# A planned four-layer graph-attention kernel: the first graph's start in tiles and plain products, and due times as priorities

## The chip, the cores and the metric

The kernel runs on one core of a Trainium2 chip. The metric is device time in microseconds (us) of one execution, and lower is better. "PE" is TensorE, "DVE" VectorE, "ACT" ScalarE, "POOL" GpSimd and "SP" SyncE, which here only issues transfers. All arithmetic is float32, except for adjacency codes in bf16 and 16-bit halves of float32 numbers that are moved as raw bits.

## The reference

There are 32 independent graphs (`B = 32`) of 512 nodes (`N`) with 256 features (`H`), each with a 512x512 adjacency matrix of integers. Each graph passes through four residual layers, one after another. Every layer normalises its input first:

```python
h = jnp.maximum(_layernorm(x, axis=-1), 0.0)
x = x + layer(h, adj, weights)
```

Layer 0 is what the change touches. Its attention matrix is used twice:

```python
q = einsum('bnh,hk->bnk', h, att_W)
score = einsum('bnk,bmk->bnm', q, h) / sqrt(H)
att = softmax(score + mask)            # mask from adj
for W, b in ((W0, b0), (W1, b1)):
    h = tanh(att @ (h @ W + b))
```

Layers 1 and 2 are graph attention with additive scores (a leaky ReLU of a source term plus a target term, masked, softmax or normalised exponentials, times the projected features). Layer 3 has bilinear scores, a softmax and two more products.

## The kernel before

**Tiles.** A graph's `x` is held as four tiles of 128 nodes (`NT = 4`), and features as two chunks of 128 (`HC = 2`). For a product PE needs the normalised features turned, as `hT` (features on partitions). In `normed` (L464 and on) DVE takes the statistics of a tile (`stats`, L470 and L471) and the variance of two tiles (`variance`, L474), POOL raises it to the power -1/2 (`root`, L477), DVE makes an offset (`offset`, L480), and ACT applies both (`norm`, L484). Then DVE splits the tile into two planes of 16-bit halves (`split`, L489), a transposing transfer on SP's queue turns them (`turn`, L492) and ACT joins the halves into `hT` (`join`, L497).

**Seven products for eight.** Layer 0's features `fa0` (`features_t`, PE L676), values `v0` (`by_nodes`, PE L702) and similarities `q0` (`scores0`, PE L729) are each computed as a 2x2 block product with seven multiplications (`seven`). For this DVE forms block sums of the operands (`block_sums`, L561: `hs` and `fs`), the weights are laid out in seven blocks (`seven_of`, L343 to L348), and partial results are added up: L691 for `fa`, L714 and L719 for `v`, L746 for `q`. Then come the exponential (ACT L737 or L743), the mask (DVE L752), `attend` (PE `bank_a`, L659: attention times values, in two groups of four steps), tanh (ACT L765), and the second convolution (`bank_z` L774, `bank_o` L792). The next layer's first product is `bank_v` (L591). Layer 3 uses the same scheme (`f3`, `v3`, `s3`, `w3`).

**The plan.** No loop over graphs is executed in order. `graph(b, ...)` only records operations, each with an engine, a cost (how long it holds the engine, and how long until its result is there), the operations it comes after, and the buffers it uses (35 pages, 8 PSUM banks, one adjacency buffer, and so on). `Plan.order` then plays the costs through: whenever an engine is free it takes the ready operation of lowest rank whose buffers are free. The result is written out as one fixed instruction order per engine. `Plan.best` tries several spacings between graphs (`APART`) and keeps the shortest plan. Five graphs are in flight at a time. The rank before is

```python
o["rank"] = ((o["graph"] - late) * apart + late * apart_last - o["way"], o["number"])
```

where `way` is the longest path of costs from the operation to the end of its own graph; paths that lead into another graph do not count. On the chip only the order stands; what an instruction waits for are the tiles that it reads or overwrites.

**Transfers.** SP's queue holds the loads of `x` (`fetch_x`, L437, 512 KB at once), of the adjacency (`fetch_adj`, L440, 256 KB each, one after another) and the transposing transfers of `code` (L452) and of the planes (L492). ACT's queue starts with `b0` (L365), `att_W` and `W0` (L367). All other weights are loaded by POOL (`load`, L290) and prepared by PE (`transposed`, L310; `product`, L327) and DVE (L313, L331). In the plan each transfer has a fixed duration, and transfers do not slow each other.

Of the kernel before, what the change touches and what calls it, by code (L numbers as in the profile page):

```python
# [19 lines left out]
P = 128  # L20
# [28 lines left out]
D_X, D_ADJ, D_ADJ0 = (550.0, 5000.0), (550.0, 12000.0), (550.0, 2500.0)  # L49
# [3 lines left out]
class Plan:  # L53
# [9 lines left out]
    APART, APART_LAST = [1000.0 * k for k in range(32, 64, 2)], [1000.0 * k for k in (2, 8)]  # L63
    SLACK = {"V": (1.05, 0.0), "A": (1.05, 0.0), "G": (1.5, 0.0), "D": (1.0, 800.0)}
# [4 lines left out]
    def op(self, engine, cost, after, emit, graph, uses=()):  # L69

        much, more = self.SLACK.get(engine, (1.0, 0.0))
        cost = cost[0] * much, cost[1] * much + more
        flat = []
        for a in after:
            flat += a if isinstance(a, tuple) else [a]
        o = {"engine": engine, "cost": cost, "after": [a for a in flat if a is not None], "emit": emit,
             "graph": graph, "uses": list(uses), "number": len(self.ops)}
        self.ops.append(o)
        return o
# [6 lines left out]
    def best(self, pools):  # L86
        apart = min(itertools.product(self.APART, self.APART_LAST), key=lambda a: self.order(pools, *a)[1])
        out, took = self.order(pools, *apart)
        assert len(out) == len(self.ops), "the plan is stuck"
        return out, took  # L90

    def order(self, pools, apart, apart_last):
        free = {pool: list(range(n)) for pool, n in pools.items()}
        users = {}
        for o in self.ops:
            o["left"], o["way"] = len(o["after"]), 0.0
            for p in o["uses"]:
                p["users"] = 0
                p.pop("number", None)
            for a in o["after"]:  # L100
                users.setdefault(a["number"], []).append(o)
# [4 lines left out]
        for o in reversed(self.ops):  # L106
            o["way"] += o["cost"][1] + self.PASS
            late = max(0, o["graph"] - last + 2)
            o["rank"] = ((o["graph"] - late) * apart + late * apart_last - o["way"], o["number"])
            for a in o["after"]:  # L110
                if a["graph"] == o["graph"]:
                    a["way"] = max(a["way"], o["way"])
# [8 lines left out]
        now, out = 0.0, []  # L121
        while True:
            for e in engines:
                skipped = []
                while at[e] <= now and ready[e]:
                    rank, o = heapq.heappop(ready[e])
                    new = [p for p in o["uses"] if "number" not in p]
                    need = [p["pool"] for p in new]
                    if any(len(free[n]) < need.count(n) for n in need):
                        skipped.append((rank, o))  # L130
                        continue
                    for p in new:
                        p["number"] = free[p["pool"]].pop(0)
                    holds, until = o["cost"]
                    at[e] = now + holds
                    out.append(o)
                    heapq.heappush(events, (at[e], next(numbers), None))
                    heapq.heappush(events, (now + until + self.PASS, next(numbers), o))
                for x in skipped:
                    heapq.heappush(ready[e], x)  # L140
# [19 lines left out]
def kernel(  # L160
# [118 lines left out]

    W = Tiles("w")  # L280

    def prepare(engine, cost, after, emit, *keys):
        return plan.op(engine, cost, after, emit, 0, W.uses(keys))

# [3 lines left out]
    def load(dst, src, *keys):  # L288

        return prepare("G", G_LOAD, [], lambda: nc.gpsimd.dma_start(out=dst() if callable(dst) else dst, in_=src), *keys)  # L290
# [73 lines left out]
    w0_sb, att_sb = raw("raw9"), raw("raw10")  # L364
    nc.scalar.dma_start(out=b0_sb, in_=line_of(b0))  # L365
    for n, dst, w, key in (("att", att_s, att_w, "raw10"), ("w0", w0_s, w0, "raw9")):
        a = prepare("A", (500.0, 4000.0), [], lambda w=w, key=key: nc.scalar.dma_start(out=raw(key)(), in_=rows_of(w)), key)  # L367
        ready[n] = seven_of(raw(key), dst, HALF, [a], key)
# [45 lines left out]
    def graph(b, adj_before, x_before):  # L414
# [4 lines left out]
        def op(engine, cost, after, emit, *keys):  # L419
            return plan.op(engine, cost, after, emit, b, T.uses(keys))  # L420
# [15 lines left out]
        def fetch_x():  # L436
            nc.sync.dma_start(out=T["x"], in_=x[b].rearrange("(t p) h -> p t h", p=P))  # L437
# [4 lines left out]
        got_x = op("D", D_X, [x_before], fetch_x, "x", "ahead")  # L442
        got_adj = [adj_before]
        for t in range(NT):

            got_adj.append(op("D", D_ADJ if b else D_ADJ0, got_adj[-1:], partial(fetch_adj, t), "adj"))
# [18 lines left out]
        def normed(l, xs):  # L465
# [28 lines left out]

            def join(t):
# [5 lines left out]
            for g in range(NT // 2):  # L501
# [4 lines left out]
                for t in (2 * g, 2 * g + 1):  # L506
                    flat, over = f"planes{l}_{t}", f"planesT{l}_{t}"
                    a = op("A", A_NORM, [r], partial(norm, t), "x", f"xn{l}")
                    a = op("V", V_SPLIT, [a], partial(split, t), f"xn{l}", flat)
# [95 lines left out]
        def leaky_exp_t(l, ss, sign):  # L605
# [35 lines left out]
            else:  # L641
                a = op("V", V_SQUARES, ss, squares, f"sT{l}")
                a = op("D", D_OUT, [a], collect, f"sT{l}")
                a = op("D", D_SPREAD, [a], spread, key)
# [59 lines left out]


        hs = normed(0, [got_x] * NT)
        right_after, right = block_sums("hs0", "hT0", lambda j, l, T=T: T["hT0"][:, j, half(l)], hs, left=False)
        qs = features_t(0, right_after, right, att_s, ready["att"])

        def block_v0(i, l):  # L710
            return T["v0"][:, two(l), LEAD + i * HALF : LEAD + (i + 1) * HALF]

        def write_v0(i, l, key, start, after):
            return op("V", V_SUM, after, lambda: nc.vector.tensor_tensor(  # L714
                block_v0(i, l), two_tiles(key, start, HALF),
                b0_sb[:, i * HALF : (i + 1) * HALF].unsqueeze(1).to_broadcast([P, 2, HALF]), ALU.add), key, "v0")

        def add_v0(i, l, key, start, after):
            return op("V", V_SUM, after, lambda: nc.vector.tensor_tensor(  # L719
                block_v0(i, l), block_v0(i, l), two_tiles(key, start, HALF), ALU.add), key, "v0")  # L720

        vs = seven("v0", pe(nt=4), lambda x, after=right_after: after(x) + ready["w0"], ("hT0", "hs0"),
                   partial(by_nodes, w0_s, right), write_v0, add_v0, beside=N // 2)
        vs = [tuple(vs.values())] * NT
        left_after, left = block_sums("fs0", "fa0", lambda i, j: T["fa0"][:, j, half(i)], qs, left=True)

        def scores0(right, left, x, p, fresh):
            for j in range(2):
                nc.tensor.matmul(p[:, j * N // 2 : (j + 1) * N // 2], right(x)[:, j * P : (j + 1) * P], left(x),  # L729
                                 start=fresh and j == 0, stop=True, skip_group_check=True)  # L730


        def block_e0(i, l):
            return T[f"e0_{l}"][:, :, half(i)]

        def exp0(i, l, key=None):
            nc.scalar.activation(block_e0(i, l), two_tiles(key, 0, N // 2) if key else block_e0(i, l), AF.Exp,  # L737
                                 scale=float(H) ** -0.5)

        def write_q(i, l, key, start, after):  # L740
            if (i, l) == (1, 0):
                return op("A", A_COPY, after, partial(exp0, i, l, key), key, f"e0_{l}")
            return op("A", A_COPY, after, lambda: nc.scalar.copy(block_e0(i, l), two_tiles(key, 0, N // 2)), key, f"e0_{l}")  # L743

        def add_q(i, l, key, start, after):
            a = op("V", V_MASK, after, lambda: nc.vector.tensor_tensor(  # L746
                block_e0(i, l), block_e0(i, l), two_tiles(key, 0, N // 2), ALU.add), key, f"e0_{l}")
            exps.append(op("A", A_EXP, [a], partial(exp0, i, l), f"e0_{l}"))
            return exps[-1]

        def masked0(i, l):
            nc.vector.tensor_tensor(block_e0(i, l), block_e0(i, l), T["mask0"][:, two(l), half(i)], ALU.mult)  # L752

        exps = []
        qb = seven("q0", pe(n256=4), lambda x, right_after=right_after, left_after=left_after: right_after(x) + left_after(x),
                   ("hT0", "hs0", "fa0", "fs0"), partial(scores0, right, left), write_q, add_q)
        es = {il: op("V", V_MASK, [a, m0], partial(masked0, *il), "mask0", f"e0_{il[1]}") for il, a in qb.items()}
        es = [(es[0, c // 2], es[1, c // 2]) for c in range(NT)]

# [257 lines left out]
        op("G", G_STORE, last, store, "y3", "slot", "ahead")  # L1017
        return code, got_x

    code, got_x = None, None  # L1020
    for b in range(B):
        code, got_x = graph(b, code, got_x)
# [37 lines left out]
```

## Time and profile before

| | |
|---|---|
| Median of 3 timed runs | 2427.62 us (2426.65 to 2427.65) |
| The profiled execution's own time | 2423.93 us |
| Its span, from the first to the last instruction | 2422.2 us |
| Busy share of the span: PE, DVE, ACT, POOL | 98%, 85%, 71%, 10% |
| DMA, mean over the span | 73 GB/s |

The durations below are from the profiled execution. Its span lies 1.7 us below its own time and 5.4 us below the median of the timed runs, so a change of the span is carried over to the median as a difference. A matmul in float32 shows as two records (two passes). Their recorded ends are modelled and overlap the next one: the cost of a pass on a busy PE is the distance between starts, for example 0.87 us for the four passes of one `bank_a` step, and not the recorded 0.38 us each.

### The profile page before, as it was taken

What the parts mean: (1) busy time and instruction counts of PE and PEld (TensorE: products, weight loads), DVE (VectorE), ACT (ScalarE), POOL (GpSimd) and SP (SyncE); (2) the same over time, 40 slices, a digit from 0 to 9 for tenths busy, and PEclk for the clock granted to TensorE, in tenths of its full rate; (3) what the DMA queues carried; (4) which work ended last, traced back from release to release, by engine and by line L of the source; (5) the groups of instructions that cost most, each with busy time, mean ns of one, the idle gap of its engine ahead of it and who ended that gap; (6) DMA issues with size and microseconds to landing.
All of it is one profiled execution on the core that took longest, in us unless ns stands there. A gap on an engine that the chain in (4) does not pass through costs nothing.

```text
span 2422.2 us, 36547 instructions
## 1 busy us (share of the span) xinstructions
PE 2372.1 (98%) x11660; PEld 1988.7 (82%) x11660; DVE 2059.8 (85%) x6333; ACT 1727.2 (71%) x3393; POOL 252.0 (10%) x320
## 2 busy tenths in 40 slices
PE   6999999999999999999999999999999999999998
PEld 5777788888888888888888888888888888887877
DVE  6677888888988888988888988889888898886888
ACT  3666767777777777777777777777777777665885
POOL 2000101010101010011001011001010110000110
PEclk9999999999999999999999999999999999999999
DMA  6222333324333333333233333333333333320221
GB/s 165 58 53 64 74 68 92 75 62 88 77 77 85 72 63 83 77 79 77 67 78 77 76 83 70 64 85 77 77 82 75 62 92 76 73 49 18 49 44 44
DMA packets 431761, 176.08 MB, mean 73 GB/s; under 512 B 387952, under 2 KB 404976, under 8 KB 431568
## 3 DMA queue, kind: packets, MB, share of 16 engines
q1 hardware_dynamic: 425520, 154.33, 29.9%
q0 software_dynamic: 5360, 18.75, 2.5%
q8 instruction: 92, 1.51, 0.3%
q14 instruction: 101, 0.83, 0.1%
q10 hardware_dynamic: 688, 0.66, 0.1%
HBM read 64.49 MB, written 16.87 MB: 34 GB/s over the span
## 4 chain that ended last, share of the span: by engine, by line
PE 88%; ACT 4%; DVE 3%; issue 3%; DMA 1%; POOL 0%; ACTq 0%; POOLq 0%; DVEq 0%
PE bank_a L659 34%; PE bank_z L774 9%; PE bank_v L591 8%; PE bank_o L792 4%; PE bank_q0p L729 4%; PE bank_s3p L906 4%; PE bank_f0p L676 4%; PE bank_v0p L702 4%; PE bank_w3p L702 3%; PE bank_f3p L676 3%; PE bank_q0q L729 3%; PE bank_s3q L906 3%; PE bank_v3p L702 2%; PE bank_v3q L702 2%; ACT xn L484 1%
## 5 line engine op out<-in xcount | busy, mean ns | idle before, releaser
L659 PE MATMUL bank_a<-v,e 128*128 128x257 f32 (+1 forms) x4096 | 976.1, 381 | 7.9 <-ACT e L632 2.7
L659 PEld LDWEIGHTS bank_a<-v,e 128*128 128x128 f32 x4096 | 757.7, 190 | 158.9 <-issue 49.6
L497 ACT COPY hT<-planesT 128x512 uint16<-128x512 uint16 x512 | 383.4, 768 | 76.0 <-DMA planesT<-planes 75.6
L477 POOL TENSOR_TENSOR rstd<-ve,mhalf 128x2 f32<-128x2 f32 x256 | 215.6, 854 | 1965.8 <-DVE ve L474 1656.3
L484 ACT ACTIVATE xn<-x,off,rstd 128x256 f32<-128x256 f32 x512 | 279.3, 593 | 33.1 <-DVE off L480 32.9
L489 DVE COPY planes<-xn 128x512 uint16<-128x512 uint16 x512 | 210.6, 423 | 52.8 <-DMA planesT<-planes 39.4
L591 PE MATMUL bank_v<-l_aug,hT 128*128 128x258 f32 x1024 | 250.0, 381 | 1.7 <-ACT hT L497 1.6
L774 PE MATMUL bank_z<-e,y 128*128 128x512 f32 x512 | 240.7, 592 | 0.1
L591 PEld LDWEIGHTS bank_v<-l_aug,hT 128*128 128x128 f32 x1024 | 192.3, 190 | 32.2 <-ACT hT L497 4.0
L470 DVE BATCH_NORM_STATS2 st<-x 128x6 f32<-128x256 f32 x512 | 209.2, 409 | 0.0
L635 ACT ACTIVATE e<-e 128x512 f32<-128x512 f32 x256 | 153.1, 626 | 0.0
L774 PEld LDWEIGHTS bank_z<-e,y 128*128 128x128 f32 x512 | 95.4, 190 | 67.9 <-issue 57.4
L598 ACT COPY v<-bank_v 128x256 f32<-128x256 f32 x256 | 90.9, 375 | 58.8 <-PE bank_v L591 50.4
L792 PE MATMUL bank_o<-w_sb,zT 128*128 128x256 f32 x512 | 120.5, 379 | 0.0
L632 ACT ACTIVATE e<-row,scores 128x512 f32<-128x512 f32 x176 | 117.6, 711 | 0.0
L913 DVE SCALAR_TENSOR_TENSOR e<-bank_s3p,v,mask 128x256 f32<-128x256 f32 x256 | 111.2, 476 | 6.9 <-PE bank_s3p L906 6.8
L686 ACT ACTIVATE fa<-bank_f3p,l_u 128x256 f32<-128x256 f32 x128 | 60.6, 473 | 74.3 <-PE bank_f3p L676 71.9
L471 DVE BATCH_NORM_AGGREGATE mv<-st 128x2 f32<-128x6 f32 x512 | 93.2, 182 | 17.5
L792 PEld LDWEIGHTS bank_o<-w_sb,zT 128*128 128x128 f32 x512 | 96.4, 190 | 13.9 <-DVE st L470 0.2
L737 ACT ACTIVATE e<-e 128x512 f32<-128x512 f32 x96 | 60.6, 631 | 50.7 <-DVE e L746 50.0
L800 ACT ACTIVATE z<-z 128x512 f32<-128x512 f32 x64 | 40.2, 629 | 74.3 <-DVE z L796 74.2
L815 DVE TENSOR_TENSOR e<-e,mask 128x512 f32<-128x512 f32 x128 | 83.4, 685 | 8.0 <-ACT e L635 7.6
(175 smaller groups left out, 4524.0 us busy)
## 6 DMA issues: line engine op xcount, KB each, us to landing
adj<-in_adj_dram SPq DMA_DIRECT2D x128, 256.0 KB
x<-in_x_dram SPq DMA_DIRECT2D x32, 512.0 KB
out_dram<-y POOLq DMA_DIRECT2D x32, 512.0 KB, 3.9
row<-row SPq DMA_DIRECT2D x44, 256.0 KB
planesT<-planes SPq DMA_TRANSPOSE x512
codeT<-code SPq DMA_TRANSPOSE x128
crest<-crest SPq DMA_TRANSPOSE x64
raw_w<-in_L_gnn_W_dram POOLq DMA_DIRECT2D x3, 256.0 KB, 9.2
```

Of the source, the lines that this page charges most:

```text
L470: nc.vector.bn_stats(T[f"st{l}"][:, t, :], T["x"][:, t, :])
L477: nc.gpsimd.tensor_tensor(T[f"rstd{l}"][:, two(g)], T[f"ve{l}"][:, two(g)], mhalf[:, two(g)], ALU.pow)
L484: nc.scalar.activation(T[f"xn{l}"][:, t, :], T["x"][:, t, :], AF.Relu, bias=T[f"off{l}"][:, t : t + 1], scale=T[f"rstd{l}"][:, t : t + 1])
L489: nc.vector.tensor_copy(T[f"planes{l}_{t}"], bits)
L497: nc.scalar.copy(bits[:, :, :, t * P : (t + 1) * P], T[f"planesT{l}_{t}"].rearrange("p (b c) n -> p b c n", b=2))
L591: nc.tensor.matmul(T[key][:, :cols], T[f"hT{l}"][:, c, t * P : (t + 1) * P], w_aug[:, c, :], start=(c == 0), stop=(c == HC - 1))
L659: nc.tensor.matmul(T[keys[j]][:, : LEAD + H + 1 - lead], e(l, c)[:, t * P : (t + 1) * P], T[f"v{l}"][:, c, lead:], start=(c == 0), stop=(c ...
L676: nc.tensor.matmul(p[:, : N // 2], w[:, x - 1, :], right(x), start=fresh, stop=True, skip_group_check=True)
L702: nc.tensor.matmul(p[:, j * k : (j + 1) * k], right(x)[:, j * P : (j + 1) * P], w[:, x - 1, :], start=fresh and j == 0, stop=True, skip_gr ...
L729: nc.tensor.matmul(p[:, j * N // 2 : (j + 1) * N // 2], right(x)[:, j * P : (j + 1) * P], left(x), start=fresh and j == 0, stop=True, skip ...
L774: nc.tensor.matmul(T[f"bank_z{k}"], T["y0"][:, c, k * P : (k + 1) * P], e(0, c), start=(c == 0), stop=(c == NT - 1))
L792: nc.tensor.matmul(T[key][:, j * H : (j + 1) * H], T["zT"][:, k, t * P : (t + 1) * P], w1_sb[:, k, :], start=(k == 0), stop=(k == HC - 1))
```

## The change

There are three edits.

1. **Graph 0 starts in another way.** Its `x` is loaded in four transfers, one for each tile. Its layer-0 features are turned by PE (`turn_pe`, two transposes for each tile through the identity) and copied from PSUM by DVE (`out_of`). Its `fa0`, `v0` and `q0` are plain products, with the weights as loaded: no block sums and no partial results. Its adjacency loads no longer wait for each other. All other layers and graphs stay as they were.
2. **The plan's ranks are due times.** An operation's due time is the smallest over its users, of any graph, minus their costs; before, the path ended at the border of the graph. The load of `x` comes after that of two graphs earlier, not of one.
3. **The plan's transfers share a way.** A transfer with a size takes its turn on a common wire of 200 bytes a nanosecond and lands 2 us later. In the plan POOL's weight loads come after graph 0's last adjacency load. On ACT's queue `b0` is issued first, then a one-element exponential (`warm`), then `att_W` and `W0`.

```diff
-D_X, D_ADJ, D_ADJ0 = (550.0, 5000.0), (550.0, 12000.0), (550.0, 2500.0)
+D_X, D_ADJ = (550.0, 5000.0), (550.0, 5000.0)
+    LAND, RATE = 2000.0, 200.0
...
-        for o in reversed(self.ops):
-            o["way"] += o["cost"][1] + self.PASS
+        for o in self.ops:
             late = max(0, o["graph"] - last + 2)
-            o["rank"] = ((o["graph"] - late) * apart + late * apart_last - o["way"], o["number"])
+            o["due"] = (o["graph"] - late) * apart + late * apart_last
+        for o in sorted(self.ops, key=lambda o: -o["depth"]):
+            o["due"] -= o["cost"][1] + self.PASS
+            o["rank"] = (o["due"], o["number"])
             for a in o["after"]:
-                if a["graph"] == o["graph"]:
-                    a["way"] = max(a["way"], o["way"])
+                a["due"] = min(a["due"], o["due"])
...
+                    if o["size"]:
+                        wire = max(wire, now) + o["size"] / self.RATE
+                        until = wire - now + self.LAND + o["late"]
...
+    warm = const.tile([P, 1], F32, tag="warm", name="warm")
+    nc.scalar.activation(warm, zero, AF.Exp)
...
-        got_x = op("D", D_X, [x_before], fetch_x, "x", "ahead")
+        got_x = [op("D", D_X, [x_before], partial(fetch_x, ts), "x", "ahead", size=P * H * 4 * (ts.stop - ts.start))
+                 for ts in ([slice(t, t + 1) for t in range(NT)] if b == 0 else [slice(0, NT)])]
...
+        if b == 0:
+            for o in loads:
+                o["after"] += got_adj[-1:]
...
+            def turn_pe(t, key):
+                for c in range(HC):
+                    nc.tensor.transpose(T[key][:, c * P : (c + 1) * P], T[f"xn{l}"][:, t, c * P : (c + 1) * P], ident)
+
+            def out_of(t, key):
+                nc.vector.tensor_copy(T[f"hT{l}"][:, :, t * P : (t + 1) * P], T[key][:, : HC * P].rearrange("p (c n) -> p c n", c=HC))
...
+                    if b == l == 0:
+                        key = f"bank_n{t}"
+                        a = op("PE", pe(nt=2 * HC), [a], partial(turn_pe, t, key), f"xn{l}", key)
+                        done.append(op("V", V_ADD, [a], partial(out_of, t, key), f"hT{l}", key))
+                        continue
...
+        if b == 0:
+            qs, vs, es = [], [], []
+            for k in range(HC):
+                key = f"bank_f0{k}"
+                def features(k, key):
+                    for c in range(HC):
+                        nc.tensor.matmul(T[key], att_sb()[:, c, k * P : (k + 1) * P], T["hT0"][:, c, :],
+                                         start=(c == 0), stop=(c == HC - 1))
...
+            for t in range(NT):
+                key = f"bank_v0{t}"
+                def values(t, key):
+                    for c in range(HC):
+                        nc.tensor.matmul(T[key][:, :H], T["hT0"][:, c, t * P : (t + 1) * P], w0_sb()[:, c, :],
+                                         start=(c == 0), stop=(c == HC - 1))
...
+            for c in range(NT):
+                key = f"bank_q0{c}"
+                def similar(c, key):
+                    for k in range(HC):
+                        nc.tensor.matmul(T[key], T["hT0"][:, k, c * P : (c + 1) * P], T["fa0"][:, k, :],
+                                         start=(k == 0), stop=(k == HC - 1))
...
     for b in range(B):
-        code, got_x = graph(b, code, got_x)
+        code, got = graph(b, code, got_x[-2])
+        got_x.append(got)
```

In the built order of the changed kernel, PE's queue begins with graph 0: three pairs of transposes, the values of tile 0, the fourth pair, the values of tiles 1 and 2, the features (`bank_f0`), the values of tile 3, one small weight product (`bank_w<-l_ac,raw_w`, layer 1's), the similarities (`bank_q0`) and then `bank_a`. The other weight preparation stands between later instructions. DVE's queue begins with the seven blocks of `att_W`, the statistics of tiles 0 and 1, the blocks of `W0`, and then tiles 2 and 3. POOL's queue has graph 0's two `root` steps ahead of all weight loads.

## The prediction

> **What bounds the kernel now.** I read the page's head first, then busy time by stages, then PE's waits, then the first 100 us in order of time.
>
> ```profile
> span 2422.2 us, 36547 instructions
> ...
> PE 2372.1 (98%) x11660; PEld 1988.7 (82%) x11660; DVE 2059.8 (85%) x6333; ACT 1727.2 (71%) x3393; POOL 252.0 (10%) x320
> ```
>
> PE is busy 98% of the span: only about 50 us are idle. Where do they lie? In the stages below the columns are length, then busy time of PE, PEld, DVE, ACT and POOL, then clock, DMA share and GB/s.
>
> ```profile
> 0.00:50.00 50.00, 28.11 (x129) 23.68 (x130) 31.98 (x123) 18.09 (x33) 15.67 (x38) 0.97 0.74 185
> 50.00:120.00 70.00, 69.96 (x328) 56.07 (x327) 49.63 (x149) 41.40 (x82) 4.64 (x6) 1.00 0.28 60
> 120.00:300.00 180.00, 174.21 (x831) 141.78 (x830) 143.48 (x446) 123.53 (x250) 16.72 (x21) 1.00 0.29 64
> 300.00:2100.00 1800.00, 1790.69 (x8824) 1507.84 (x8823) 1567.14 (x4824) 1322.70 (x2591) 186.57 (x221) 1.00 0.35 77
> 2300.00:2422.20 122.20, 110.32 (x590) 94.45 (x588) 106.73 (x304) 84.78 (x170) 9.42 (x11) 0.98 0.18 44
> ```
>
> PE idles 21.9 us in the first 50 us, nothing until 120 us, 5.8 us until 300, 9.3 us in the next 1800, 11.9 us at the end. A steady part that is 99.5% full can give almost nothing; the start can. PE's waits in the first 120 us name it:
>
> ```profile
> PE bank_w L310 <- DMA raw_w<-in_L_gnn_W_dram: 13.3, 1, 13.3
> PE bank_w L327 <- DVE raw_w L313: 6.2, 1, 6.2
> ```
>
> In order of time (start, duration, engine, line; in brackets the idle time before and what ended it):
>
> ```profile
> 8.45 1.28 ACT L484 ACT_TABLE_LOAD   x1 [8.45 <-DMA x<-in_x_dram]
> 9.87 0.29 DVE L343 COPY att_s<-raw_w 128x256 f32<-128x256 f32 x1 [8.99 <-DMA raw_w<-in_L_gnn_att_W_dram]
> 14.11 0.30 DVE L343 COPY w_s<-raw_w 128x256 f32<-128x256 f32 x1 [2.88 <-DMA raw_w<-in_L_gnn_W_dram]
> 15.38 0.42 DVE L470 BATCH_NORM_STATS2 st<-x 128x6 f32<-128x256 f32 x1
> 19.61 2.22 ACT L484 ACTIVATE xn<-x,off,rstd 128x256 f32<-128x256 f32 x4 [9.88 <-DVE off L480]
> 27.79 0.77 ACT L497 COPY hT<-planesT 128x512 uint16<-128x512 uint16 x1 [5.96 <-DMA planesT<-planes]
> 35.18 1.02 PE L676 MATMUL bank_f0p<-hT,att_s 128*128 128x256 f32 x2
> 55.83 1.03 PE L659 MATMUL bank_a<-v,e 128*128 128x257 f32 x4
> 98.73 1.03 PE L591 MATMUL bank_v<-l_aug,hT 128*128 128x258 f32 x4
> ```
>
> `x` is there at 8.45, but DVE's queue holds its statistics behind the blocks of `W0` until 15.38; normalising takes until 21.8; split, transfer and join until 34.3; the first attention step runs at 55.83.
>
> **The measure.** Call lag the start of an instruction minus the work ahead of it in PE's queue, each pass at its full-speed distance between starts (0.43 us for 512 columns, 0.216 for 256, 0.11 for 128 or less). Before the first `bank_a` stand 26.6 us of work (9.6 weight preparation, 11.3 of graph 0, 5.7 of graphs 1 and 2): lag 55.8 - 26.6 = 29.2. Before the first `bank_v` stand 69.6: lag 98.7 - 69.6 = 29.1. The lag is made by the first `bank_a` and then stays. If PE stays fed, the end moves by the change of the lag plus that of the work.
>
> **Work added to PE.** Graph 0, layer 0: features 8 passes of 512 for 14 of 256, 3.45 for 3.02; values 16 of 256 for 28 of 128, 3.46 for 3.11; similarities 16 of 512 for 28 of 256, 6.91 for 6.05; transposes 16 of 128, 1.76. Sum +3.4 us, all on the bound engine.
>
> **Work taken from others.** DVE loses eight block sums and six partial sums of `fa` and `v` (0.42 each) and three of `q` (0.68); four copies out of PSUM (0.42) stand for four splits (0.42): 7.9 us less. ACT loses four joins (0.77) and some copies. SP's queue loses four transfers of planes (1.19 to issue) and gains three of `x` (0.46 to 0.57 each). These are off the path after the start, and I count them at nothing; they are covered by PE's own work.
>
> **The chain of the start.**
> - `att_W`. DVE's first real instruction still waits for it. Before it landed at 9.87 beside POOL's loads, which now come later; but its issue moves from 1.19 behind a 1.28 us table load, and behind it on ACT's queue stands `W0`. DMA had moved 0.95 MB by 7.0 us (sum of the GB/s by microsecond); `b0`, graph 0's `x` and `att_W` are 0.9 MB. I take 7.3, between 6.5 and 9.9.
> - DVE: blocks 1.4 (9.87 to 11.23), statistics of two tiles 1.05, blocks of `W0` 1.4, tile 2 and `variance` 0.7: 11.8. POOL's `root` 0.85: 12.7. Two `classes` (0.69 each, L449) stand between the two offsets: 13.3 and 14.1. They wait for the adjacency; if the last load lands after 13.3, the second offset waits with it. Normalising ends at 15.7, against 21.8.
> - PE starts near 14.0, against 13.3, but with graph 0's own work. It was slow when it began: the `bank_w` products of L327 start 0.44 us apart in place of 0.216, and the granted clock was 0.50 from 34 to 36 us. So I take transposes and three values at half speed, 8.7 us in place of 4.4, less 1 us at the end for a clock that may open by then: PE is through at about 21.7. DVE's copies of `hT` (0.42 each, with statistics of graph 1 between) are done near 19 and hidden by this.
> - Features 3.45, the second copy of `fa` on ACT 0.6, semaphores 0.3: similarities from 26.0. At full speed all the way it would be 23.3 (the copies of `hT` set it then); at half speed to the end, 30.
> - The small weight product ahead of them waits for two POOL loads. POOL is free of `root` at 13.6; the fourth load's issue ends at 16.6. The like loads landed 9.1 us after issue in the crowd before, 3.3 and 5.6 when it was over: 20 to 25.7. I take 22, hidden by the features; if the cover is gone, it costs up to 1 us, and far more only if those loads slip beyond 26.
> - Similarities 6.9: 32.9. Exponential 0.63 and mask 0.69 follow each tile, and DVE has statistics of graphs 2 to 4 between the masks. The masks come at about 29.0, 30.8, 33.3 and 35.1, so the last steps of `bank_a` are held up about 1 us.
>
> The first `bank_a` at 32.9 with 16.0 us of work ahead is a lag of 16.9; the weight products fill the gaps after it. Taking 1.5 us for thinner cover later (five graphs begin with 13 us less lead, DVE was 97% busy from 40 to 60), the lag falls by 29.2 - 16.9 - 1.5 = 10.8. With the 3.4 us of added work: -7.4 us. At full speed all the way (2.7 less) and `att_W` at 6.5 (0.8 less) it is -10.9. I take the middle, -9, since the values have gaps between them that half speed only fills.
>
> The Trainium skill, "TensorE: Matmul & The Clock Gate", section "The HAM clock gate", says that the clock opens after some 3.4 us of sustained activity; its section "PE-mode transpose" says that transposes do not count as busy in the same way, which speaks against turning the features on PE. By that the gate would open one window after the values start, before the features, and the sum would be near -8; no row here shows the two kinds apart in the cold state.
>
> **Ranks and shared way.** In the built order graphs 6 to 25 still follow each other every 72.6 us of PE work, and the last 50 instructions of PE are those of before. The closest distance between a scored value and its attention (`bank_v` to `bank_a`, layer 1) falls from 17.8 to 14.4 us of PE work for one graph. So I take nothing, with bounds of -3 (a third of the 9.3 us idle) and +6 (0.2 us for each graph).
>
> **Rivals.**
> - *Late operands* (no full gain): clock at half through the similarities (+3.4 for half of them) and `l_ac` at 25.7 (+0.7), with thinner cover 3 us more: about -2, 2425.5. For it: the row of 0.50 came after 8 us of PE work in the 10 us before. Against: that work had gaps and one- and two-column products.
> - *The tiles do not help*: `att_W` at 9.87 and `W0` at 14.11 as now. Then the statistics of tile 2 start at 15.4, everything moves by 3.6 us, -5, 2422.5. For it: both loads are issued later. Against: POOL's 1.3 MB are out of the way.
> - *Slower by the ranks*: due times that look across graphs put `classes`, adjacency and `x` of later graphs ahead of chain work in the steady part. DVE (87% busy there) and ACT (73%) serve in order, so each such step delays a chain by 0.4 to 0.7 us. One uncovered step of 0.7 for each of 26 graphs is +18, in sum +9, 2436.5. It decides from 0.35 us for each graph. Against: the distances above.
>
> **The numbers.** Forecast 0.60 (-4 to -14), late operands 0.17, no help from tiles 0.11, slower by ranks 0.12. The profiled span would be 2413; on the median 2427.6 - 9 = 2418.6. About 0.2% (4.9 us) is what a measurement of this kernel can tell from no change. Faster by more: nearly all of the forecast, half of the third case, a third of the second, 0.68; within: 0.20; slower: 0.12. The range takes the forecast's 2413.6 with 2 us for bounds, up to 2428: it leaves out the slower case and little else.
>
> **What the profile after would show.** Right: the first transposes near 14, the first `bank_q0` near 26, the first `bank_a` near 33, PE over 99% busy from 50 to 120 us and idle about 9 us from 300 to 2100. Wrong: DVE's first block after 10 us, a wait of PE for `bank_w<-l_ac,raw_w` of over 3 us, PE under 95% from 40 to 120, or over 15 us idle in the steady part.

## The result, and the profile after

The changed kernel takes 2413.25 us (median of 4 runs, 2412.41 to 2414.35), the kernel before 2427.14 (4 runs, 2425.81 to 2427.65): a ratio of 0.9944, 95% interval 0.9927 to 0.9961. The profiled execution took 2412.91 us, its span is 11.1 us shorter than before. The medians lie 13.9 us apart: the profiled execution before (2423.93) was 3.2 us faster than its median, the one after 0.3 us.

The page's head:

```profile
span 2411.1 us, 36568 instructions
...
PE 2370.4 (98%) x11638; PEld 1983.9 (82%) x11638; DVE 2052.5 (85%) x6316; ACT 1720.6 (71%) x3385; POOL 262.3 (11%) x320
```

Busy time by stage (columns as for the kernel before):

```profile
0.00:50.00 50.00, 35.81 (x134) 24.13 (x135) 33.54 (x129) 23.16 (x44) 19.08 (x42) 1.00 0.76 200
50.00:120.00 70.00, 68.50 (x331) 55.85 (x330) 54.23 (x163) 39.23 (x77) 4.25 (x6) 1.00 0.42 98
120.00:300.00 180.00, 179.25 (x866) 147.76 (x865) 143.56 (x444) 126.59 (x255) 14.78 (x18) 1.00 0.25 51
300.00:2100.00 1800.00, 1787.63 (x8803) 1504.11 (x8802) 1565.33 (x4822) 1320.25 (x2591) 195.93 (x222) 1.00 0.35 76
2300.00:2411.10 111.10, 99.23 (x535) 84.80 (x533) 97.24 (x272) 73.78 (x148) 8.09 (x10) 0.97 0.19 45
```

PE's idle time falls from 21.9 to 14.2 us in the first 50 us and from 5.8 to 0.8 between 120 and 300; it rises from 0 to 1.5 in between and from 9.3 to 12.4 in the steady part. The two long waits for weights are gone from the first 120 us; what is left is the wait for graph 0's own features:

```profile
PE bank_n L523 <- ACT xn L510: 13.5, 1, 13.5
```

The start in order of time:

```profile
1.19 1.28 ACT L389 ACT_TABLE_LOAD   x1 [1.19 <-PEq L1124]
1.25 0.41 ACTq L384 DMA_DIRECT2D raw_w<-in_L_gnn_att_W_dram  x1
6.81 0.29 DVE L361 COPY att_s<-raw_w 128x256 f32<-128x256 f32 x1 [5.93 <-DMA raw_w<-in_L_gnn_att_W_dram]
9.17 0.26 DVE L361 COPY w_s<-raw_w 128x256 f32<-128x256 f32 x1
13.46 1.67 PE L523 MATMUL bank_n<-ident,xn 128*128 128x128 f32 x6 [13.46 <-ACT xn L510]
17.05 3.13 PE L764 MATMUL bank_v<-raw_w,hT 128*128 128x256 f32 x8
20.02 3.60 PE L754 MATMUL bank_f<-hT,raw_w 128*128 128x512 f32 x8
24.68 7.11 PE L775 MATMUL bank_q<-fa,hT 128*128 128x512 f32 x16
31.63 1.03 PE L698 MATMUL bank_a<-v,e 128*128 128x257 f32 x4
```

`att_W` is there at 6.81 for 9.87, `W0` no longer holds DVE, and the first `bank_a` runs at 31.63 for 55.83: with 16.0 us of PE work ahead of it, a lag of 15.6 for 29.2.

**How transposes count.** The work ahead counts each transpose on PE as two passes of 0.11 us, here as in the prediction. The trace has one record for each (the x6 above are three pairs), and on a busy PE at full speed the next start is 0.109 us later. So the eight transposes of graph 0 add 0.9 us and not 1.76, and the work added is 2.5 us and not 3.4. The lags below keep the prediction's count so that they can be held against it; with single passes the first `bank_a` has a lag of 16.5 for 30.4. Where this changes a reading, the text gives both.

Lag can be followed through the whole program: take the first start of each stretch of PE's order from the trace, and subtract the work ahead of it. The table has the kernels of the experiments as well, but for `start_warm`, whose extra products shift the count; "planned apart" is the spacing between graphs that the planner picked, or was given.

| kernel | planned apart, us | lag at 100 us of PE work | at 300 | rise from 400 to 1900 | rise from 1900 to 2330 | median, us |
|---|---|---|---|---|---|---|
| before | 40 | 28.8 | 36.3 | 20.1 | 10.2 | 2427.14 |
| changed | 40 | 17.4 | 18.1 | 24.9 | 8.8 | 2413.25 |
| after_38 | 38 | 17.9 | 23.0 | 33.6 | 10.0 | 2426.17 |
| old_ranks | 38 | 17.0 | 22.2 | 31.5 | 7.9 | 2423.18 |
| blocks_late | 38 | 14.2 | 18.4 | 33.6 | 10.1 | 2422.53 |
| x_whole | 38 | 19.0 | 25.6 | 32.5 | 10.0 | 2430.19 |
| seven_first | 38 | 22.6 | 28.8 | 33.0 | 10.5 | 2432.47 |
| dma_turn | 38 | 24.4 | 30.2 | 32.9 | 10.4 | 2433.15 |
| loads_early | 38 | 17.5 | 29.6 | 33.0 | 10.6 | 2434.38 |
| common_start | 42 | 32.6 | 35.7 | 20.9 | 12.7 | 2427.69 |
| before_42 | 42 | 30.2 | 37.5 | 8.0 | 9.0 | 2416.26 |
| start_alone | 42 | 19.4 | 25.2 | 8.3 | 9.3 | 2405.38 |
| start_loads | 42 | 20.0 | 23.4 | 8.9 | 8.7 | 2404.24 |

For the change: the lag at 300 is 18.2 us lower, the steady part gives back 5.0 (from 300 to 1900), the end is 1.4 better, and 3.4 of work is added: 18.2 - 5.0 + 1.4 - 3.4 = 11.2, the 11.1 of the spans. (The double count is in the lag and in the work alike, and drops out of this sum.)

### The profile page after: what moved, and what is told of

The parts are those of the page before. It is cut to its first block, busy times and chain, and to the rows that moved or that the text cites. A ratio compares the mean times of both kernels' runs of the same rounds, so it can differ in the third digit from the quotient of the medians.

```text
span 2411.1 us, 36568 instructions
## 1 busy us (share of the span) xinstructions
PE 2370.4 (98%) x11638; PEld 1983.9 (82%) x11638; DVE 2052.5 (85%) x6316; ACT 1720.6 (71%) x3385; POOL 262.3 (11%) x320
## 4 chain that ended last, share of the span: by engine, by line
PE 90%; issue 3%; ACT 3%; DVE 2%; DMA 2%; SPq 0%; POOL 0%; POOLq 0%; DVEq 0%; ACTq 0%
PE bank_a L698 35%; PE bank_z L851 9%; PE bank_v L630 8%; PE bank_o L869 5%; PE bank_q0p L806 4%; PE bank_s3p L983 4%; PE bank_v0p L741 4%; PE bank_f0p L715 4%; PE bank_w3p L741 4%; PE bank_f3p L715 4%; PE bank_q0q L806 3%; PE bank_s3q L983 3%; PE bank_v3p L741 2%; PE bank_v3q L741 2%; DMA planesT<-planes 1%
## 5 line engine op out<-in xcount | busy, mean ns | idle before, releaser
L503 POOL TENSOR_TENSOR rstd<-ve,mhalf 128x2 f32<-128x2 f32 x256 | 223.0, 884 | 1947.7 <-DVE ve L500 1668.9
L515 DVE COPY planes<-xn 128x512 uint16<-128x512 uint16 x508 | 206.6, 422 | 19.1 <-DMA planesT<-planes 13.7
L496 DVE BATCH_NORM_STATS2 st<-x 128x6 f32<-128x256 f32 x512 | 210.1, 410 | 0.0
L671 ACT ACTIVATE e<-row,scores 128x512 f32<-128x512 f32 x176 | 118.0, 711 | 13.9 <-DMA row<-row 13.7
L497 DVE BATCH_NORM_AGGREGATE mv<-st 128x2 f32<-128x6 f32 x512 | 93.2, 182 | 17.5
L869 PEld LDWEIGHTS bank_o<-w_sb,zT 128*128 128x128 f32 x512 | 96.5, 190 | 13.9 <-DVE st L496 0.2
L829 DVE TENSOR_TENSOR e<-e,mask 128x512 f32<-128x512 f32 x124 | 85.0, 686 | 9.4 <-ACT e L814 9.3
L892 DVE TENSOR_TENSOR e<-e,mask 128x512 f32<-128x512 f32 x128 | 84.0, 688 | 5.4 <-ACT e L674 5.1
```

Of the source, the lines that this page charges most:

```text
L496: nc.vector.bn_stats(T[f"st{l}"][:, t, :], T["x"][:, t, :])
L503: nc.gpsimd.tensor_tensor(T[f"rstd{l}"][:, two(g)], T[f"ve{l}"][:, two(g)], mhalf[:, two(g)], ALU.pow)
L515: nc.vector.tensor_copy(T[f"planes{l}_{t}"], bits)
L869: nc.tensor.matmul(T[key][:, j * H : (j + 1) * H], T["zT"][:, k, t * P : (t + 1) * P], w1_sb[:, k, :], start=(k == 0), stop=(k == HC - 1))
```

## The experiments

The experiments were timed in three groups, each on another chip and with the kernel before beside it: `old_ranks`, `common_start`, `dma_turn` and `seven_first` (before: 2425.87 us); `x_whole`, `loads_early`, `start_alone` and `blocks_late` (2426.02); and the other four (2426.38). Differences of one or two us between groups therefore say little.

**old_ranks**: the ranks of before, everything else changed.

```diff
-            o["due"] -= o["cost"][1] + self.PASS
-            o["rank"] = (o["due"], o["number"])
+            o["way"] += o["cost"][1] + self.PASS
+            o["rank"] = ((o["graph"] - late) * apart + late * apart_last - o["way"], o["number"])
             for a in o["after"]:
-                a["due"] = min(a["due"], o["due"])
+                if a["graph"] == o["graph"]:
+                    a["way"] = max(a["way"], o["way"])
```

> The changed kernel with the ranks of before (longest path inside the own graph); its start, its shared way and its loads stay. PE's order is then nearly that of the changed kernel: graphs 72.6 us of PE work apart, 16.0 us of work ahead of the first bank_a. Theory A (the gain comes from graph 0's start alone): first bank_a at 31.6 us as in the changed kernel, time 2413, within 2 us. Theory B (the due times are what emptied the idle time of 5.8 us between 120 and 300 us): that idle time comes back, 2417 to 2418. Theory C (the due times cost the 3 us that PE idles more between 300 and 2100 us, 12.4 for 9.3): these go, 2410.

2423.18 us, ratio to before 0.9990 (0.9981 to 0.9999): far beyond what any of the three allowed. The start is that of the changed kernel (lag 17.0 at 100), but the steady part loses 31.5 us for 24.9. That looked like a price of the old ranks, until the next five kernels, which keep the new ranks, lost as much.

**common_start**: graph 0 on the path of all other graphs.

```diff
-                 for ts in ([slice(t, t + 1) for t in range(NT)] if b == 0 else [slice(0, NT)])]
+                 for ts in [slice(0, NT)]]
...
-                    if b == l == 0:
+                    if False:
...
-        hs = normed(0, got_x if b == 0 else got_x * NT)
-        if b == 0:
+        hs = normed(0, got_x * NT)
+        if False:
```

> The changed kernel with graph 0 on the path of all other graphs (x in one load, features turned by transfers, seven products for eight); due times, shared way, later POOL loads and the order on ACT's queue stay. PE has 3.4 us less work. Theory A: all is in graph 0's start. The lag of the first bank_a (its start less the PE work ahead, 24.0 us here) goes back from 15.6 to near 29, less up to 3.6 us because W0 lands earlier than before: 13.6 - 3.6 - 3.4 = +6.6 at least, +10.2 at most, so 2420 to 2423.5. Theory B (ranks and the shared way carry the gain): 2411 to 2414.

2427.69 us, ratio 1.0009 (1.0000 to 1.0017). Without graph 0's start, due times and shared way, at the 42 us that the planner picks for them, gain nothing. PE's first work comes at 22.3 us, since its weights now come late and it has nothing else, so the lag at 100 is 3.8 above that of before, not below.

**dma_turn**, **seven_first**, **x_whole**, **loads_early**: one part of the new start undone in each. `dma_turn` turns graph 0's features by transfers:

```diff
-                    if b == l == 0:
+                    if False:
```

`seven_first` gives its layer 0 back to seven products:

```diff
         hs = normed(0, got_x if b == 0 else got_x * NT)
-        if b == 0:
+        if False:
```

`x_whole` loads its `x` at once:

```diff
-                 for ts in ([slice(t, t + 1) for t in range(NT)] if b == 0 else [slice(0, NT)])]
+                 for ts in [slice(0, NT)]]
...
-        hs = normed(0, got_x if b == 0 else got_x * NT)
+        hs = normed(0, got_x * NT)
```

`loads_early` lets POOL's loads go first:

```diff
-        if b == 0:
-            for o in loads:
-                o["after"] += got_adj[-1:]
```

> The changed kernel, but graph 0's layer-0 features are turned by transfers, as in the other graphs (four splits on DVE, four transposing transfers, four joins on ACT); tiles of x and plain products stay. PE has 1.8 us less work; 17.8 us of it lie ahead of the first bank_a. In the profile before, 6.0 us of idle ACT lay between the last splits and the joins. If turning by PE carries its part: features 5 to 8 us later, less 1.8 of work and less the slow-clock stretch of the values (they start with all operands there): +2 to +6, 2415 to 2419. If the transfers were hidden by the rest of the start: -1.8, 2411.5.

> The changed kernel, but graph 0's layer 0 uses seven products for eight (block sums and partial sums on DVE); x in tiles and the turn by PE stay. PE has 1.7 us less work, 19.7 us lie ahead of the first bank_a. DVE gains eight block sums and six partial sums of 0.42 us and three of 0.68, of which some 4 to 6 us stand between hT and the last similarity. If the plain products carry their part: +2 to +4, 2415 to 2417. If the block sums lie beside PE's work: -1.7, 2411.5.

> The changed kernel with graph 0's x in one load of 512 KB instead of four of 128 KB. Before, the one load ended at 8.45 us; in the changed kernel DVE's statistics of tile 0 start after the blocks of att_W, which land at 6.8 us. In this order DVE takes all four tiles' statistics ahead of the blocks of W0. If the tiles carry a part: x lands after att_W, statistics begin up to 1.5 us later, +0.5 to +1.5, 2414 to 2415. If att_W alone sets the start: 0, 2413, or a little less, since W0's blocks (1.4 us) no longer stand between the tiles: down to -1.4, 2412.

> The changed kernel, but POOL's weight loads do not come after graph 0's last adjacency load in the plan, so they are issued from the first microseconds on, as before. If the crowd of loads is what held att_W (9.87 us before, 6.81 changed) and W0 (14.1 before): att_W lands 2 to 3 us later and W0 3 to 5, so everything at the start moves by 3 to 4 us: 2416 to 2417. If the loads were in nobody's way (the order on ACT's queue did it): 2413.

2433.15, 2432.47, 2430.19 and 2434.38 us: all slower than the kernel before (ratios 1.0030, 1.0026, 1.0015 and 1.0034, the lowest end of an interval 1.0006), and 17 to 21 us above the changed kernel, where at most 6 had been expected. At 100 us of work they had lost 7.0, 5.2, 1.6 and 0.1 us of lag (with single passes for transposes 6.1, 4.9, 1.8 and 2.7); the rest came later. All four, with `old_ranks` and `blocks_late`, had one thing in common: the planner had picked 38 us between graphs, not 40, and their middle graphs have one and the same order on PE, DVE and ACT. Hence `after_38` below, against which their times can be read.

The traces also say what each part does at the start. `att_W`, in `x_whole`, `loads_early` and, for the adjacency that DVE's `classes` wait for, `loads_early` again:

```profile
9.73 0.29 DVE L361 COPY att_s<-raw_w 128x256 f32<-128x256 f32 x1 [8.85 <-DMA raw_w<-in_L_gnn_att_W_dram]
```

```profile
6.91 0.51 DVE L361 COPY att_s<-raw_w 128x256 f32<-128x256 f32 x1 [6.04 <-DMA raw_w<-in_L_gnn_att_W_dram]
...
16.29 0.75 DVE L472 TENSOR_SCALAR code<-adj 128x1024 bf16<-128x1024 int32 x1 [4.14 <-DMA adj<-in_adj_dram]
```

With `x` in one load `att_W` comes at 9.73, as before; with the tiles at 6.91, though POOL's loads are early again. So the tiles brought `att_W` forward, and the late loads something else: the adjacency, for which DVE waited until 16.29 with the second `offset` behind it. In the changed kernel that `code` runs at 11.94 without a wait.

**start_alone**: the new start with the ranks, the durations of transfers, the chain of `x` loads and the early loads of before.

```diff
-D_X, D_ADJ = (550.0, 5000.0), (550.0, 5000.0)
+D_X, D_ADJ, D_ADJ0 = (550.0, 5000.0), (550.0, 12000.0), (550.0, 2500.0)
...
-                    if o["size"]:
-                        wire = max(wire, now) + o["size"] / self.RATE
-                        until = wire - now + self.LAND + o["late"]
...
-            got_adj.append(op("D", D_ADJ, got_adj[-1:] if b else [], partial(fetch_adj, t), "adj", size=P * N * 4))
+            got_adj.append(op("D", D_ADJ if b else D_ADJ0, got_adj[-1:] if b else [], partial(fetch_adj, t), "adj", size=P * N * 4))
...
-        code, got = graph(b, code, got_x[-2])
+        code, got = graph(b, code, got_x[-1])
```

(and the edits of `old_ranks` and `loads_early`)

> The first of the three edits alone: graph 0's x by tiles, turned by PE, plain products; ranks, the durations of transfers in the plan, the chain of x loads and POOL's early loads are those of before, and only b0 and the one-element exponential ahead of att_W on ACT's queue stay. Theory A with the loads in the way: the gain of the start less 3 to 4 us for the crowd, 2416 to 2418. Theory A without: 2413. Theory B (ranks and shared way carry the gain): 2421 to 2425. If the new ranks or the shared way cost the 3 us more idle in the steady part: 2410.

2405.38 us, ratio 0.9915 (0.9901 to 0.9928): better than the changed kernel and than every expectation. The start is later (lag 19.4 at 100, 25.2 at 300), but the steady part loses 8.3 us for 24.9. Its planner had picked 42.

**blocks_late**: the seven blocks of `att_W` and `W0`, which graph 0 no longer uses, out of the way of its statistics.

```diff
         hs = normed(0, got_x if b == 0 else got_x * NT)
+        if b == 0:
+            for o in ready["att"] + ready["w0"]:
+                o["after"] += hs
```

> The changed kernel with the seven blocks of att_W and of W0 put after graph 0's features are turned: its plain products do not use them, yet they stood first in DVE's queue, so that the statistics waited for att_W until 6.8 us and then for 1.4 us of blocks, and for 1.4 us more between tiles 1 and 2. If DVE's queue sets the start: normalising 2 to 3.5 us earlier, PE starts near 11 for 13.5, 2410 to 2411. If the clock of PE sets it (an earlier start is only run at half speed for longer) or the POOL roots do: 0 to -1, 2412 to 2413.

2422.53 us (38 us apart): 3.6 below `after_38`, so the edit is worth what was expected of it, at another spacing. PE began at 9.60 and stood again until 12.86: DVE's copies of `hT` were now behind a `code` that waited 2.68 us for the adjacency.

```profile
12.86 2.08 PE L767 MATMUL bank_v<-raw_w,hT 128*128 128x256 f32 x4 [2.08 <-DVE hT L526]
```

**after_38** and **before_42**: one number in each, the spacing that the planner may pick.

```diff
-    APART, APART_LAST = [1000.0 * k for k in range(32, 64, 2)], [1000.0 * k for k in (2, 8)]
+    APART, APART_LAST = [38000.0], [1000.0 * k for k in (2, 8)]
```

(42000.0 in `before_42`)

> The changed kernel with one number fixed: graphs are planned 38 us apart, not the 40 that the planner picked for it (and for the kernel before). The six kernels of this study whose planner picked 38 (old_ranks, dma_turn, seven_first, x_whole, loads_early, blocks_late) have the same order of instructions for a middle graph on PE, DVE and ACT, and so has this one. Between 400 and 1900 us of PE work they lose 31.5 to 33.6 us, the changed kernel 24.9, the kernel before 20.1. If the spacing makes that loss: +7 to +9 in the steady part, 2420 to 2423, the same as old_ranks within 2 us (then the ranks are worth nothing). If the loss came from the parts that were undone: 2413.

> The kernel before with one number fixed: graphs are planned 42 us apart, not 40; the planner holds this plan to be 0.4 us longer. Its middle graphs have the same order as start_alone, which lost 8.3 us between 400 and 1900 us of PE work where the kernel before lost 20.1. If the order of the steady part makes that loss: 12 us less, 2413 to 2417, as much as the whole change. If the loss comes from what the start hands down: 2425 to 2428.

2426.17 us and 2416.26 us (ratios 1.0001, 0.9992 to 1.0010, and 0.9955, 0.9943 to 0.9968). The changed kernel planned 38 us apart loses its whole gain, 12.9 us; the kernel before planned 42 apart gains 10. The planner holds 38 to be 2.0 us longer than 40 for the one, and 42 to be 0.4 longer than 40 for the other: it can't see differences of 10 us that the chip makes. PE's longest waits from 300 to 2100 us (total, times, longest), in the kernel before, the changed kernel, `after_38` and `before_42`:

```profile
PE bank_f0p L676 <- ACT fa L684: 5.2, 11, 0.5
```

```profile
PE bank_f0p L715 <- ACT fa L723: 7.0, 17, 0.5
```

```profile
PE bank_v0p L741 <- DVE v L791: 6.7, 22, 0.3
PE bank_f3p L715 <- ACT fa L725: 4.0, 21, 0.6
PE bank_w3p L741 <- DVE w L1055: 2.9, 19, 0.2
```

```profile
PE bank_a L659 <- DVE e L842: 1.4, 1, 1.4
PE bank_a L659 <- ACT e L958: 1.2, 2, 0.8
```

Each order has waits of its own, which in the first three come back from graph to graph: a partial product waits until DVE or ACT has read the PSUM bank (one of the eight buffers for PE's results) that it will overwrite. At 42 us this view shows none that repeats. The waits cost more than they show, because recorded ends overlap the next start; in the changed kernel:

```profile
1121.39 0.61 PE L741 MATMUL bank_v3p<-l_aug,hT 128*128 128x129 f32 x4
1122.47 0.70 PE L715 MATMUL bank_f0p<-hs,att_s 128*128 128x256 f32 x2 [0.47 <-ACT fa L723]
```

Four passes of 0.11 would have ended at 1121.83: PE lost 0.64 us, and the first pass after it took 0.1 longer, where 0.47 shows as idle.

The starts give the whole of it. From 400 to 1900 us of work, take each distance between starts less the distance that such passes have when nothing is waited for. What is left over is 18.0 us before, 22.8 changed, 31.5 in `after_38` and 6.0 in `before_42`, and 17.5, 22.4, 30.2 and 6.0 of it stand at the first passes of partial products. `bank_f0p` alone makes 14.2 before and 16.1 changed; `bank_v0p`, `bank_f3p` and `bank_w3p` make 29.9 in `after_38`. The order at 42 has such a pause too, one in each graph at `bank_f0p`, but of only 0.29 us. So what the spacing moves is these pauses.

**start_loads**: `start_alone` with late loads (its diff without that of `loads_early`; planned 42 apart). **start_warm**: the same, with twelve products that nobody reads ahead of graph 0's transposes.

```diff
+        if b == 0:
+            def busy():
+                for _ in range(12):
+                    nc.tensor.matmul(T["bank_busy"][:, :H], ident, T["x"][:, 0, :], start=True, stop=True)
+
+            op("PE", (5000.0, 5170.0), got_x[:1], busy, "x", "bank_busy")
         hs = normed(0, got_x if b == 0 else got_x * NT)
```

> start_alone with POOL's loads planned after graph 0's last adjacency load, graphs 42 us apart as there: old ranks, old durations of transfers, the new start whole. If the steady order decides and the loads were in the way: first bank_a at 32 us for 37.0, the loss of the steady part still near 8 us, 2398 to 2402. If the 5 us are given back before 300 us (in start_alone the lag rose from 19.4 to 27.1 there): 2405.

> start_loads with twelve products of 256 columns on tile 0 of x, which nobody reads, ahead of graph 0's transposes: 5.2 us of work for PE while it waits, to raise its clock before its own work begins. In the changed kernel the passes were half as fast from 13.46 to 19.5 us, which cost 3 us. If PE's work before opens the clock: 1.5 to 3 us less than start_loads. If what holds up the start is DVE's copies, or the clock opens later all the same (in dma_turn 8.5 us after the first of its products, which ran without a gap): 0 to 0.5 less.

2404.24 us (2404.02 to 2405.95, ratio 0.9911, 0.9896 to 0.9926) and 2405.90 us (2403.18 to 2407.45, 0.9914, 0.9901 to 0.9928). `start_loads` has the lowest median here, 9 us below the changed kernel, but cannot be told from `start_alone`, and of the two times expected it is near the second. Its steady part is as expected (8.9); its first `bank_a` comes at 37.05, not 32. In the old plan's durations graph 0's adjacency arrives early, so DVE's queue holds `code` ahead of the statistics, and there it waits:

```profile
12.05 0.69 DVE L473 TENSOR_SCALAR code<-adj 128x1024 bf16<-128x1024 int32 x1 [3.86 <-DMA adj<-in_adj_dram]
```

In the shared way the statistics stand first and PE starts at 13.46 for 17.63: for the start it is the better plan by 4 us. The idle products of `start_warm` bought nothing:

```profile
5.48 8.39 PE L747 MATMUL bank_busy<-x,ident 128*128 128x256 f32 x24 [5.48 <-DMA x<-in_x_dram]
17.89 1.67 PE L521 MATMUL bank_n<-ident,xn 128*128 128x128 f32 x6 [4.02 <-ACT xn L508]
```

Their passes went from 0.43 to 0.22 us at 11.5, so they did raise the clock; 4.0 us of idle time followed, and from 18.3 us the transposes and the first values ran at 0.21 and 0.43 again, until 21.8.

Read against `after_38`, which has the same order of middle graphs, the parts are worth: late loads 8.2 us (2434.38), the turn by PE 7.0, plain products 6.3, tiles of `x` 4.0; `blocks_late` would add 3.6. `old_ranks` is 3.0 faster, but its ratio to before (0.9981 to 0.9999) overlaps that of `after_38` (0.9992 to 1.0010) and its middle graphs have the same order: a price of the due times is not shown. The four parts add up to more than the new start brings as a whole (12.0 us, `start_loads` against `before_42`; 10.9 without late loads, `start_alone`). Part of them can be PE's clock: in the profiled executions the granted clock fell to 0.50 from 198.9 to 205.7 us in `x_whole`, from 206.7 to 210.1 in `loads_early`, and from 35.9 to 39.3 and 203.2 to 206.6 in `seven_first`, while in `after_38` it stayed at 1.00 from 18.2 to 2332 us. A stretch of 3.4 us at half clock costs up to 1.7 us. How much of a part's price is the delay itself, how much the clock, and how much other delays that then surface, was not separated.

## Why the prediction was right

- **Bound.** The start could give, and gave: at 100 us of PE work the lag is 11.4 us lower, with the 3.4 of work -8.0 (with single passes 10.1 and 2.5, -7.6), where the sum said -7.4 and I took -9. `start_alone` against `before_42`, with the same order of middle graphs, shows it in the time: 10.9 us.
- **`att_W`** came at 6.8, taken 7.3 (6.5 to 9.9), but for another reason than I gave: not POOL's late loads, but the tiles of `x` (9.73 in `x_whole`, 6.91 in `loads_early`). Nor was its issue behind the table load: it ran at 1.25, within it.
- **PE** started at 13.46, not 14.0. Half speed ended at 19.55, in the third value, so transposes and three values took 6.6 us for the 7.7 I counted. The transposes were counted twice (3.5 us at half speed, for 1.9 from starts), and the clock opened later than I took, only 0.5 us before the features. Similarities ran from 24.68 for 26.0, and the first `bank_a` from 31.63 for 32.9, without a hold-up by the masks. The small weight product waited for nothing, as taken.
- **Thinner cover.** From the first `bank_a` to 100 us of work the lag rose from 15.6 to 17.4, and with single passes from 16.5 to 20.3 (not at all before); 1.5 was taken. So this term was some 2 us too small. PE was 97.9% busy from 50 to 120 us, not over 99%.
- **From 100 to 300 us of work**, which the prediction held to be carried on unchanged ("and then stays"), the kernel before loses 7.5 us and the changed one 0.7 (with single passes 10.4 and 3.1). This term was missing: about 7 us of gain, though the profile before had shown 5.8 us of idle PE there. The loss differs from order to order: 7.3 in `before_42`, 3.4 in `start_loads`, 3.1 in `common_start`, 5.1 in `after_38`. Which edit brings the gain is not settled.
- **Ranks and shared way** were taken at nothing (-3 to +6). The steady part costs 5.0 us from 300 to 1900: this is the term that was mis-sized, the one that my slower rival priced. It isn't the due times that make it: at 38, 40 and 42 us apart, old ranks and due times give the same built order for a middle graph on PE, DVE and ACT. The shared way, with the longer chain of `x` loads, changes that order, and at 42 us apart it costs more: 20.9 (`common_start`) for 8.0 (`before_42`). I had weighed the distance from a scored value to its attention and the work per graph; the waits that repeat are for PSUM banks of partial products, which stood in neither.
- **Sum.** In the span the forecast was only 2.1 us off (9 for 11.1), since two terms of 5 to 7 us that I did not have are of opposite sign and nearly cancel: that is luck. The median is 5.4 us lower than forecast (2413.25 for 2418.6). Of this 2.9 come from the profiled executions, which were faster than their medians by 3.2 us before and by 0.3 after, so that the change of the span does not carry over as it stands. It is luck too that the planner picked 40 us for the changed kernel and not 38, by 2.0 us of planned time: at 38 the same change gains nothing (2426.17). The signs named for the start held; idle time in the steady part was 12.4, not 9.
- **Rivals.** Late operands and tiles of no help are refuted by the rows above: the clock opened before the features, and `x_whole` costs 4.0 us. Slower by ranks has the right place (the order of the steady part) and the wrong part.
- **Clock.** PE's passes reached full speed 6.1 us after its first transpose here. In `dma_turn`, whose stretch has values, passes of two columns and weight transposes without a gap, it was 8.6 us (21.83 to 30.4). In `start_alone` it was 3.2 us (20.51 to 23.74), of which 2.2 were transposes; the passes of the values behind them went from 0.43 to 0.22 us apart after the third (rows below). The Trainium skill, "TensorE: Matmul & The Clock Gate", sections "The HAM clock gate" and "PE-mode transpose", says some 3.4 us of sustained activity, and that transposes do not count as busy in the same way. No run here shows that the transposes held the clock back: the stretch that begins with ten of them reached full speed soonest. In the other two the time to full speed was longer than the page's.

```profile
20.51 1.18 PE L518 MATMUL bank_n<-ident,xn 128*128 128x128 f32 x4 [6.37 <-ACT xn L505]
21.48 0.63 PE L326 MATMUL bank_w<-ident,l_aug 128*128 128x128 f32 x2
21.91 1.06 PE L518 MATMUL bank_n<-ident,xn 128*128 128x128 f32 x4
22.76 2.38 PE L759 MATMUL bank_v<-raw_w,hT 128*128 128x256 f32 x8
```

## What to carry to other kernels

Where a planner writes the order out, a change at the start also draws a new steady order, and that can be worth as much as the change: here one number, the spacing, moved the time by 10 to 13 us, in cases where the planner saw 0.4 and 2. Follow the start of work less the work ahead through the whole program, compare parts only between kernels with the same steady order, and try the planner's near ties on the chip before the change itself is judged.

## What the runs showed of the hardware

- A transfer on ACT's queue was issued at 1.25 us, during ACT's own table load (1.19 to 2.47).
- With 512 KB of `x` in one transfer, `att_W` on another queue was there at 9.5 to 9.9 us; with the same `x` in four transfers at 6.7 to 6.9, with or without POOL's loads beside it.
- PE's passes took twice as long for the first 3.2 us (`start_alone`, after a short burst earlier), 4.3 (`start_loads`), 4.9 (`after_38`), 6.1 (the changed kernel) and 8.6 us (`dma_turn`) of a stretch of work, and again after a pause of 4.0 us (`start_warm`).
- A transpose of 128x128 float32 on PE is one record, 0.109 us from the next start at full speed; a product of 128 columns is two records of 0.11 each.
